# Two attention blocks in fp32 on one core: where a batch of stores is issued, three pair transfers in two attentions, one seam's PSUM copy, and the place of the last normalise

## The chip, the cores and the metric

The kernel runs on 1 core of one Trainium2 chip. The metric is the device time of one execution in microseconds (us). The kernel before took 3185.87 us, the median of 3 runs (3183.12 to 3187.95).

## The reference

Eight images of 512 channels and 32 x 32 pixels go through two attention blocks, one after the other, each with its own weights. All is fp32.

```python
# one block; C = 512, S = 1024 positions, 8 heads of d = 64, 8 groups
xn  = group_norm(x) * gamma + beta
q, k, v = Wq xn + bq, Wk xn + bk, Wv xn + bv          # 512 x 512 each
attn = softmax(q^T k / sqrt(d))                        # per head, 1024 x 1024
out  = attn v
x    = x + Wp out + bp
```

A pair of an image and a block is called a job here; there are 16, numbered n = 0 to 15 in the order image 0 block 0, image 1 block 0, image 0 block 1, image 1 block 1, then images 2 and 3, and so on. Attention n is the attention of job n.

## The kernel before, in words

**Stages.** TensorE goes through job after job: projections, attention, then a seam into the next job. The output projection of job n is done in the seam together with the projections of job n + 1. The 512 x 512 products use a scheme with 7 products in place of 8 (`v_phase`, `deep_phases`, `last_proj`), one level deep for the first two jobs' values and the last output, two levels deep otherwise. For two levels the weights need sums of blocks ("factors"). They are made once: four times, in attentions 0, 1, 2 and 3, `deep_round` loads a weight matrix into one large SBUF tile (tag `deep`, one buffer; the profile calls it `round`), VectorE forms the factors in 4 + 4 additions (L162 to L168), and seven stores of 448 KB (L235) write them to DRAM, from where later jobs load them (`w<-deep`). The tag `deep` is used again by the next holder: in attention 0 by another raw weight load (L157, `raw`), in attentions 1 to 3 by the sums of the next input (L482 to L488).

**Attention.** There are 8 groups, one for each pair of heads (hp) and half of the query positions (sh), and 8 steps in a group, one for each chunk of 128 key positions: 64 steps of about 1.72 us of TensorE. In step i TensorE makes the scores `sc` (L1099) into one of two PSUM buffers, ScalarE the exponential `e` (L1104) into SBUF, and two steps later TensorE the product with the values (L1150, into `po`). The `e` tiles come from a pool of 12 buffers; at step 58 six of these go to the next job's weights.

**The softmax's sums.** The eight exponentials of a group have to be added. The first four are added in two pairs: a GpSimd transfer adds one exponential onto the other in SBUF (L1127, `e<-e`), and VectorE adds the result to `acc` (L1130) five steps after the issue. The other four are added by VectorE alone (L1118, then L1120). In the last group of an attention `pairs` is 0 and all eight are added by VectorE. After a group, `take` copies one half of `po` to SBUF with ScalarE (L1171) and VectorE adds it to the other half, which it reads from PSUM (L1173). With `middle` given, ScalarE copies the second half as well (L1176) and VectorE adds two SBUF tiles (L1178). `reduce` turns `acc` into row sums (L1185). After every second group the sums are gathered over partitions by three small DMAs (`r<-r`, L1208), 7.6 us later inverted (L1212, L1213, ...), written to DRAM and broadcast back (`rd`, L1225; `rb`, L1227), and 16.2 us later multiplied into the outputs (`normalise`, L1242). For the last two groups this is done on VectorE without DMAs, with times of its own.

**Side work.** `chores` and `moves` hang on step numbers: the next job's group norm (its statistics; `groups`, L331 to L341, with the DMAs `dg` and `mr`; the factors `mul` and `off`, L349 to L351; then four normalisations on ScalarE, L356, in attentions 0, 2 and 3 after steps 24, 25, 27 and 28), the sums of its blocks (L423 to L429), the factor steps and the stores above.

**What sets the order.** TensorE, ScalarE and VectorE execute in the order of the program text, with `later` and `advance` as a clock that inserts delayed steps. The queues of SP and GpSimd are ordered by the framework; each is served in order. [...]

**The last seam.** `last_proj` runs for both halves of the positions. Its chain has four PSUM tiles; the fourth product into `z_last` can start when VectorE has added the product before it to `x` (L1064) . The normalise of the last two groups (L1242) and the sums of the second half (L1018 to L1027) stand among those additions in VectorE's queue.

The few lines that place the stores in an attention (`put_round`, in `fast_path`):

```python
at = max(at + 3, 25)
for i, fn in enumerate(stores):
    at = move(at + 1 + i % 2, fn)
```

They give the steps 26, 28, 29, 31, 32, 34 and 35 in attentions 0, 2 and 3, and 30, 32, 33, 35, 36, 38 and 39 in attention 1.

Of the kernel before, what the change touches and what calls it, by code (L numbers as in the profile page):

```python
# [41 lines left out]
FACTOR = {1: A11, 2: A12, 3: S4, 4: A22, 5: S1, 6: S2, 7: S3}  # L42
# [39 lines left out]
def fast_path(  # L82
# [10 lines left out]
    nc = tc.nc  # L93
# [17 lines left out]
    jobs = [(b0 + i, layer) for b0 in range(0, B, 2) for layer in range(2) for i in range(2)]  # L111
# [4 lines left out]
    def later(delay, fn):  # L116
        todo.append((clock[0] + delay, fn))
# [25 lines left out]
    def raw_block(layer, which, i, j):  # L143

        if which == O:
            w, at = wp[layer], 0
        else:
            w, at = wqkv[layer], {Q: 0, K: C, V: 2 * C}[which]
        cols = slice(at + i * CH, at + (i + 1) * CH)
        return w[j * CH : (j + 1) * CH, cols].rearrange("(cc p) o -> p cc o", p=P)  # L150
# [8 lines left out]
    def factor(w, part):  # L159

        if part == 0:
            nc.vector.tensor_add(w[:, S1], w[:, S3], w[:, A22])  # L162
        elif part == 1:
            nc.vector.tensor_sub(w[:, S2], w[:, S1], w[:, A11])
        elif part == 2:
            nc.vector.tensor_sub(w[:, S3], w[:, A11], w[:, S3])
        else:
            nc.vector.tensor_sub(w[:, S4], w[:, A12], w[:, S2])  # L168
# [43 lines left out]
    def deep_round(which, layer):  # L212


        box = []

        def start():
            t = acts.tile([P, NW, NW, P], F32, tag="deep", name=f"round_{which}_{layer}")
            box.append(t)
            for i in range(2):  # L220
                for j in range(2):
                    nc.sync.dma_start(
                        t[:, 2 * j + i, 0:4, :].rearrange("p (cc h) o -> p cc (h o)", cc=2),
                        raw_block(layer, which, i, j),
                    )

        def outer_(part):
            factor(box[0][:, :, 0:4, :], part)

        def inner(part):  # L230
            factor(box[0].rearrange("p f a o -> p a f o"), part)

        def store(o):
            keep = wdram.tile([P, NW, P], F32, name=f"deep_{which}_{layer}_{o}")
            nc.sync.dma_start(keep, box[0][:, FACTOR[o]])  # L235
            deep[which, layer, o] = keep

        first = [lambda part=part: outer_(part) for part in range(4)]
        second = [lambda part=part: inner(part) for part in range(4)]
        return start, first, second, [lambda o=o: store(o) for o in OUTER]  # L240
# [837 lines left out]
    class Attention:  # L1078
# [41 lines left out]
                nc.vector.tensor_add(acc[g], acc[g], e)  # L1120

        def pairs(self, g):
            return 0 if g + 1 == len(self.groups) else 2

        def add_pair(self, i):
            g, kc = self.steps[i]
# [28 lines left out]
        def finish(self, g):  # L1155

            self.take(g)
            if not self.pairs(g):
                self.reduce(g)

# [15 lines left out]
        def reduce(self, g):  # L1180
            n, q, m = self.n, self.q, g % 2
            hp, sh = self.groups[g]
            if m == 0:
                self.r = small.tile([P, NQ, 2, RP], F32, tag="r", name=f"r_{n}_{g}", bufs=1)
            nc.vector.tensor_reduce(  # L1185
                self.r[:, 0, m, :], self.acc.pop(g).rearrange("p j (b e) -> p (j b) e", e=RP), AX.X,
                ALU.add, apply_transpose=True,
            )
            if m == 0:
                return  # L1190
            before = self.groups[g - 1]
            if before[0] == hp:
                place = q[:, hp, :].rearrange("p (m e) -> p m e", m=2)
            else:
                place = q[:, hp - 1 : hp + 1, sh * HALF : (sh + 1) * HALF]
            r, first = self.r, slice(0, RP)
            ends = g + 1 == len(self.groups)
            lt = small.tile([RP, 2, RP], F32, tag="lt", name=f"lt_{n}_{g}", bufs=1)
            ri = small.tile([P, 2, 2, RP // 2], F32, tag="ri", name=f"ri_{n}_{g}", bufs=1)
            box = []  # L1200

            def gather():
                for i in range(1, NQ):
                    src, to_ = r[i * RP : (i + 1) * RP, 0], r[first, i]
                    if ends:
                        nc.vector.tensor_copy(to_, src)
                    else:
                        nc.sync.dma_start(to_, src)  # L1208

            def invert():  # L1210
                inv = ri[first].rearrange("p m j b -> p m (j b)")
                nc.vector.tensor_reduce(lt, r[first].rearrange("p a m b -> p m b a"), AX.X, ALU.add)  # L1212
                nc.vector.reciprocal(inv, lt)  # L1213
                box.append(apool.tile([P, 2, HALF], F32, tag="rb", name=f"rb_{n}_{g}", bufs=1))
                if ends:
                    for i in range(1, NQ):
                        nc.vector.tensor_copy(
                            ri[i * RP : (i + 1) * RP, :, 0, :], ri[first, :, i * RP // HD, :]
                        )
                else:  # L1220
                    rt = small.tile([RP, 2, RP], F32, tag="rt", name=f"rt_{n}_{g}", bufs=1)
                    rd = dram.tile([2, 2, HALF], F32, tag="rd", name=f"rd_{n}_{g}")
                    for i in range(2):
                        nc.vector.transpose(rt[:, i, :], inv[:, i, :])
                    nc.sync.dma_start(rd.rearrange("m j (b e) -> (j b) m e", e=RP), rt)  # L1225
                    for j in range(2):
                        nc.sync.dma_start(  # L1227
                            box[0][j * HD : (j + 1) * HD],
                            rd[:, j, :].unsqueeze(0).to_broadcast([HD, 2, HALF]),
                        )  # L1230
                nc.vector.tensor_max(lmax, lmax, lt)
                nc.vector.tensor_max(rmax, rmax, inv)

            def spread():
                if ends:
                    nc.vector.transpose(
                        box[0].rearrange("p m (b e) -> p m b e", e=RP),
                        ri[:, :, 0, :].unsqueeze(3).to_broadcast([P, 2, RP // 2, RP]),
                    )

            def normalise():
                nc.vector.tensor_mul(place, place, box[0])  # L1242
                whole[0] = n if ends else -1

            times = (0.0, 7.6, 7.7, 16.2)
            if ends:
                times = (0.0, 0.2, 7.6, 8.2) if n + 1 >= DEEP_V else (0.0, 0.2, 2.0, 4.0)
                if n + 1 == len(jobs):
                    times = (0.0, 0.2, 2.0, 7.0)
            for at, step in zip(times, (gather, invert, spread, normalise)):  # L1250
                later(at, step)

# [682 lines left out]
```

## Time and profile before

| | |
|---|---|
| median of 3 runs | 3185.87 us (3183.12 to 3187.95) |
| the profiled execution | 3187.94 us, its span on the core 3186.2 us |
| TensorE busy / idle | 3156.2 / 22.8 us |
| VectorE, ScalarE, GpSimd busy | 2637.2, 2333.5, 281.0 us |
| granted TensorE clock | 0.996 |
| DMA, queues of SP and of GpSimd | 27.4% and 25.8% of 16 engines' span |

All durations in the text are from this one profiled execution. The page gives busy time per engine and groups of instructions by line. The view of waits adds up, for an engine, who ended its idle time. A timeline lists an engine's instructions in order: start and duration in us, engine, line, operation, output and input tiles, and in brackets the idle time before it and what ended that. "SPq" is SP's queue of DMA issues; the time of an issue is not the time of the transfer.

| attention | start (first exponential) | end (last exponential) |
|---|---|---|
| 0 | 81.4 us | 197.8 us |
| 1 | 294.6 us | 402.0 us |
| 2 | 492.6 us | 604.1 us |
| 3 | 692.2 us | 804.7 us |
| 4 | 892.8 us | 1000.3 us |

### The profile page before, as it was taken

The page shows a single profiled execution, that of the slowest core. Times are in us where ns is not written, and L with a number is a line of the kernel's source. Part 1 is how long each engine was busy: PE and PEld are TensorE (multiplying, and loading weights), DVE is VectorE, ACT ScalarE, POOL GpSimd, SP SyncE. Part 2 cuts the span into 40 slices and gives each one's busy share as a digit, 9 for nine tenths or more (in the row PEclk, how much of TensorE's full clock was granted, in tenths as well). Part 3 has the DMA queues.
Part 4 walks back from the last instruction along what each step waited for, and adds up shares of the span by engine and source line. Part 5 has one row for each costly group of instructions (what it writes and reads, how often), then busy time and mean ns, then how long its engine had stood idle before and what let it go on. Part 6 is the DMA issues. An engine that isn't in the chain of part 4 may idle for free.

```text
span 3186.2 us, 62139 instructions
## 1 busy us (share of the span) xinstructions
PE 3156.2 (99%) x24093; PEld 1872.4 (59%) x24093; DVE 2637.2 (83%) x3571; ACT 2333.5 (73%) x4233; POOL 281.0 (9%) x318
## 2 busy tenths in 40 slices
PE   9999999999999999999999999999999999999998
PEld 8357384573846638466393754837557375573844
DVE  8797898978879788797978969889697887978867
ACT  6648687786877868777686776867768687686863
POOL 0101101011010010100001000010000100001000
PEclk9999999999999999999999999999999999999999
DMA  7645675565745455355554545446456463544633
GB/s 276 141 124 160 153 210 140 147 192 128 213 98 146 119 110 167 75 151 159 144 184 88 159 98 138 125 94 181 131 137 182 89 201 63 136 121 96 220 78 78
DMA packets 186190, 450.31 MB, mean 141 GB/s; under 512 B 37928, under 2 KB 54176, under 8 KB 185888
## 3 DMA queue, kind: packets, MB, share of 16 engines
q1 hardware_dynamic: 137040, 296.82, 27.4%
q0 software_dynamic: 48848, 149.44, 25.8%
q8 instruction: 192, 3.15, 0.4%
q14 instruction: 110, 0.90, 0.1%
HBM read 247.41 MB, written 48.17 MB: 93 GB/s over the span
## 4 chain that ended last, share of the span: by engine, by line
PE 81%; DVE 1%; issue 0%; DMA 0%; ACT 0%; SPq 0%; POOL 0%; DVEq 0%; ACTq 0%; POOLq 0%
PE sc L1099 23%; PE po L1150 23%; PE zd L806 9%; PE vd L806 9%; PE yd L806 4%; PE ud L806 4%; PE vd L801 4%; PE zd L801 3%; PE yd L801 1%; PE ud L801 1%; DVE acc L1120 0%; PE z_last L1042 0%; DMA r<-r 0%; ACT e L1104 0%; DVE x L1064 0%
## 5 line engine op out<-in xcount | busy, mean ns | idle before, releaser
L1104 ACT ACTIVATE e<-sc 128x1024 f32<-128x1024 f32 x1024 | 1043.8, 1025 | 575.6 <-PE sc L1099 546.9
L1099 PE MATMUL sc<-q,k 64*64 64x512 f32 x8192 | 1059.2, 590 | 10.1 <-ACT e L1104 10.1
L1150 PE MATMUL po<-e,v 64*64 64x512 f32 x8192 | 1058.0, 590 | 3.4 <-ACT e L1104 3.4
L1099 PEld LDWEIGHTS sc<-q,k 64*64 64x64 f32 x8192 | 309.6, 133 | 576.7 <-issue 509.9
L1150 PEld LDWEIGHTS po<-e,v 64*64 64x64 f32 x8192 | 311.6, 133 | 572.6 <-issue 544.2
L1120 DVE TENSOR_TENSOR acc<-acc,e 128x1024 f32<-128x1024 f32 x320 | 389.4, 1217 | 39.1 <-ACT e L1104 28.9
L1127 POOL DMA_DIRECT2D e<-e x224 | 192.9, 861 | 1769.0 <-ACT e L1104 1267.8
L1118 DVE TENSOR_TENSOR acc<-e,e 128x1024 f32<-128x1024 f32 x128 | 156.4, 1222 | 147.1 <-ACT e L1104 147.1
L1130 DVE TENSOR_TENSOR acc<-acc,e 128x1024 f32<-128x1024 f32 x224 | 272.4, 1216 | 1.9
L806 PE MATMUL zd<-deep,w 128*128 128x256 f32 x860 | 240.2, 379 | 0.0
L806 PE MATMUL vd<-deep,w 128*128 128x256 f32 x804 | 223.4, 379 | 0.0
L806 PEld LDWEIGHTS zd<-deep,w 128*128 128x128 f32 x860 | 163.3, 190 | 22.5 <-ACT ud L501 0.3
L806 PEld LDWEIGHTS vd<-deep,w 128*128 128x128 f32 x804 | 152.8, 190 | 20.8
L1185 DVE TRANSPOSE_TENSOR_REDUCE r<-acc 128x32 f32<-128x1024 f32 x128 | 159.4, 1245 | 4.3
L901 POOL DMA_DIRECT2D x<-p x61 | 72.9, 1195 | 972.9 <-ACT p L823 453.9
L848 DVE TENSOR_TENSOR p<-p,s 128x512 f32<-128x512 f32 x185 | 127.2, 687 | 22.8 <-ACT p L823 19.3
L801 PE MATMUL vd<-w,deep 128*128 128x128 f32 x840 | 119.1, 275 | 1.1 <-ACT ud L501 1.1
L848 DVE TENSOR_TENSOR q<-q,s 128x512 f32<-128x512 f32 x64 | 44.1, 690 | 86.8 <-ACT q L825 45.1
L801 PE MATMUL zd<-w,deep 128*128 128x128 f32 x728 | 106.5, 275 | 0.9 <-ACT ud L501 0.9
L801 PEld LDWEIGHTS vd<-w,deep 128*128 128x128 f32 x840 | 106.2, 192 | 1.3 <-ACT ud L501 1.3
L806 PE MATMUL vd<-os,w 128*128 128x256 f32 x364 | 105.5, 379 | 0.0
L806 PE MATMUL zd<-os,w 128*128 128x256 f32 x356 | 98.9, 379 | 0.0
(296 smaller groups left out, 4826.4 us busy)
## 6 DMA issues: line engine op xcount, KB each, us to landing
w<-deep SPq DMA_DIRECT2D x399, 448.0 KB, 5.4
e<-e POOLq DMA_DIRECT2D x224, 512.0 KB, 4.7
x<-p POOLq DMA_DIRECT2D x61, 512.0 KB, 6.6
rb<-rd SPq DMA_DIRECT2D x96, 256.0 KB, 3.7
x<-x_dram SPq DMA_DIRECT2D x28, 512.0 KB, 3.7
out_dram<-x SPq DMA_DIRECT2D x28, 512.0 KB, 6.0
deep<-w SPq DMA_DIRECT2D x28, 448.0 KB, 2.7
deep<-round SPq DMA_DIRECT2D x28, 448.0 KB, 4.9
```

Of the source, the lines that this page charges most:

```text
L801: nc.tensor.matmul(ps[:, tokens], moving[i][:, tokens], lhs[:, FACTOR[i], :], start=(start and ti == 0), stop=True, skip_group_check=True,)
L806: nc.tensor.matmul(ps, lhs[:, FACTOR[i], :], moving[i], start=start, stop=True, skip_group_check=True,)
L848: nc.vector.tensor_add(to_, to_, five.to_broadcast([P, 2, QT]))
L901: nc.gpsimd.dma_start(to_, p(part), accum_op=ALU.add)
L1099: nc.tensor.matmul(sc[h * HD : (h + 1) * HD, j, :], k[r, hp, k0 : k0 + HD], q[r, hp, sh * HALF : (sh + 1) * HALF], start=True, stop=True,)
L1104: nc.scalar.activation(e, sc, AF.Exp, scale=SCALE)
L1118: nc.vector.tensor_add(acc[g], self.es[i - 1], e)
L1120: nc.vector.tensor_add(acc[g], acc[g], e)
L1127: nc.gpsimd.dma_start(self.summed[i], self.summed.pop(i - 1), accum_op=ALU.add)
L1130: nc.vector.tensor_add(self.acc[g], self.acc[g], self.summed.pop(i))
L1150: nc.tensor.matmul(po[g][j * HD : (j + 1) * HD, h, :], v[r, kc, d0 : d0 + HD], e[r, j, :], start=(kc == 0), stop=(kc == NT - 1),)
L1185: nc.vector.tensor_reduce(self.r[:, 0, m, :], self.acc.pop(g).rearrange("p j (b e) -> p (j b) e", e=RP), AX.X, ALU.add, apply_transpose=True,)
```

## The change

1. The 28 stores of `deep_round` are issued from ScalarE's queue, at their place in ScalarE's order between exponentials, in place of SP's queue.
2. In attentions 0 and 1, groups 1 to 4, three pairs are added by transfers in place of two: 8 more `e<-e` transfers; in each of these groups one L1130 more and two L1120 fewer. The reduce of these groups, and what hangs on it, comes two steps later.
3. At the end of attention 0 (the one seam where `finish` is called for the last group and another job follows), both halves of `po` are copied by ScalarE, and VectorE adds two SBUF tiles.
4. In the last seam the normalise is placed at 9.6 us of the program's clock in place of 7.0.

In the built program TensorE's order is unchanged. ScalarE's gains the 28 stores and one copy. In VectorE's, attentions 0 and 1 change: in attention 0 the factors L349 to L351 now stand before the inverse L1212. In SP's queue of attention 0 the order r<-r, seven stores, raw, rd, raw x3, rb x2, r<-r becomes r<-r, rd, rb x2, r<-r, raw x4, rd, rb x2. In the last seam L1242 moves behind the additions of `y_last` and `z_last`.

```diff
@@ deep_round, store
-            nc.sync.dma_start(keep, box[0][:, FACTOR[o]])
+            nc.scalar.dma_start(keep, box[0][:, FACTOR[o]])
@@ Attention
         def pairs(self, g):
-            return 0 if g + 1 == len(self.groups) else 2
+            if g + 1 == len(self.groups):
+                return 0
+            return 3 if self.n < 2 and 0 < g < 5 else 2
@@ finish
-            self.take(g)
+            if not self.pairs(g) and self.n + 1 < len(jobs):
+                self.take(g, lambda: None)
+            else:
+                self.take(g)
             if not self.pairs(g):
                 self.reduce(g)
@@ reduce
                 if n + 1 == len(jobs):
-                    times = (0.0, 0.2, 2.0, 7.0)
+                    times = (0.0, 0.2, 2.0, 9.6)
```

## The prediction

> **What bounds the kernel now.** I read the page's busy times first, then who TensorE waited for, then the time order of each engine around each wait.
>
> ```profile
> PE 3156.2 (99%) x24093; PEld 1872.4 (59%) x24093; DVE 2637.2 (83%) x3571; ACT 2333.5 (73%) x4233; POOL 281.0 (9%) x318
> ```
>
> TensorE is busy 3156 of 3186.2 us and nothing here removes a matmul. All that can be won is its idle time, 22.8 us. The waits of TensorE name nearly all of it:
>
> ```profile
> PE sc L1099 <- ACT e L1104: 10.1, 4, 3.4
> PE po L1150 <- ACT e L1104: 3.4, 1, 3.4
> PE v L553 <- DVE q L1173: 2.8, 1, 2.8
> ...
> PE z_last L1042 <- DVE x L1064: 1.3, 1, 1.3
> PE vd L801 <- ACT ud L501: 1.1, 1, 1.1
> PE zd L801 <- ACT ud L501: 0.9, 1, 0.9
> ```
>
> In order of time, from TensorE's timeline: S1 3.36 us at 128.4 (attention 0); S2 3.36 at 197.9 (its last step), 0.23 behind it; S3 2.77 at 209.1 (first seam); S4 0.86 and 1.09 at 416 and 421 (second seam); S5 3.00 and 0.58 at 539 (attention 2); S6 3.19 at 739 (attention 3); S7 1.34 at 3164.9 (last seam). The first 9 us hold the other 3.
>
> S1, S5 and S6 read "waits for an exponential", but the exponential stood behind a normalisation, and that behind VectorE. In the answer for L356:
>
> ```profile
> its engine sat idle before it (us, times) until:
>   DVE off L351: 12.6, 3
> ```
>
> VectorE in attention 0, at S1:
>
> ```profile
> 122.86 0.59 DVE L1212 TENSOR_REDUCE lt<-r 32x64 f32<-32x256 f32 x1 [3.10 <-DMA r<-r]
> ...
> 124.53 1.21 DVE L1120 TENSOR_TENSOR acc<-acc,e 128x1024 f32<-128x1024 f32 x1
> 125.67 0.14 DVE L349 TENSOR_TENSOR mul<-mr,vec_sb 128x4 f32<-128x4 f32 x1
> ```
>
> The factors L349 to L351 are queued behind L1212, which stands still until the gather r<-r lands. The same sequence stands at S5 and S6. Now SP's queue and the VectorE wait that follows:
>
> ```profile
> 116.69 1.84 SPq L1208 DMA_DIRECT2D r<-r  x3
> 118.58 7.85 SPq L235 DMA_DIRECT2D deep<-round  x7
> 131.17 0.38 SPq L157 DMA_DIRECT2D raw<-wqkv_dram  x1
> 131.61 0.46 SPq L1225 DMA_DIRECT2D rd<-rt  x1
> 132.11 1.45 SPq L157 DMA_DIRECT2D raw<-wqkv_dram  x3
> 134.16 2.26 SPq L1227 DMA_DIRECT2D rb<-rd  x2
> ```
>
> ```profile
> 146.70 1.23 DVE L1242 TENSOR_TENSOR q<-q,rb 128x1024 f32<-128x1024 f32 x1 [14.70 <-DMA rb<-rd]
> ```
>
> Seven stores are issued, then SP stands until they have landed (raw reuses their buffer), and rd and rb stand behind that. VectorE loses 14.7 us. I measured its lag as the start of a group's first sum (L1118) after the second exponential it reads: 0.4 us in group 1 of attention 0, 11.9 in group 3, 11.8 still in group 7 (start 195.48, exponential ended 183.65). In attention 1 it is 5.2 us at group 7, later at most 2.7. Twelve us of lag make S2: the last exponential needs the buffer which that sum frees.
>
> ```profile
> 196.79 1.02 ACT L1104 ACTIVATE e<-sc 128x1024 f32<-128x1024 f32 x1 [4.62 <-DVE acc L1118]
> ```
>
> [...] r<-r lands 0.45, 0.5 and 0.2 us after the GpSimd pair transfer then in flight (122.29, 533.09, 733.23).
>
> **The change, part by part.**
>
> *Stores by ScalarE, attention 0.* In the built order rd and rb now stand before raw, and raw comes one group later. rd is ready about 127, rb about 132 to 133 (typical landing 3.7 us), VectorE reaches L1242 at about 131. The 14.7 us wait falls to 0 to 3. What is late next is raw: the last store is issued after exponential 35, about 141, lands about 146 (median 4.9 us), raw lands about 150 to 153, VectorE wants it at about 152. A lag of 2 to 5 us is left. S2 needs a lag over about 8.5 (11.8 minus the stall 3.36). So S2 goes: -3.4, and the 0.23 behind it, -0.2; this would hold without the pairs.
>
> *Three pairs in attentions 0 and 1, groups 1 to 4.* Each adds one transfer and one L1130 and drops two L1120: one add of 1.22 us fewer, eight in all, 9.8 us of VectorE, beside TensorE. What counts is the order: group 1's reduce and its inverse move two steps (3.4 us) later, so L349 to L351 now stand ahead of L1212. They follow the group's first sum, whose exponential ends at 120.2: 120.2 + 1.2 + 0.6 = 122.0, and ScalarE wants them at 121.8. S1 goes. ScalarE then has exponentials (0.91 start to start), four normalisations (1.14) and a copy (0.46) between steps 24 and 29: by this addition exponential 26 starts 1.4 us after its scores, and TensorE bears 1.5 (2.58 us from scores to reuse, less 1.06). I take 0.15 left of 3.36: -3.2. Transfers take 25.8% of 3186 us over 285 (224 + 61), 2.9 us of all DMA engines each; three pairs in a group of 13.75 us are 63%, the stores (27.4% of 3186 us for 297 MB, so 1.35 us each) some 60% of the 15.5 us they are spread over. So for that stretch DMA is full, and transfers land up to 5 us late. A pair is wanted 5 steps, 8.6 us, after issue and lands in 4.7; its buffer is wanted 5 steps later still. That covers 5 us; if the cover is gone, each further us stops VectorE, then TensorE.
>
> *The same in attention 1.* The lag before the deep sums falls from 4.4 to about 3.5 us; the stores end at step 39, so L482, which overwrites their buffer at 42, need not wait. S4 comes from VectorE freeing small buffers late, so 0.9 less lag takes 0.8 of 1.95; bounds 0 and 2. The first store waits for the last factor step (346.56 before, about 344.5 now) and is due after exponential 30, 345.4: no wait taken. If it came 2 us later, exponential 31 behind it would be late and TensorE after it.
>
> *Attentions 2 and 3.* VectorE's order is the same, so L349 stays behind L1212. The stores stood behind r<-r on SP, not before it; they can only slow its landing. r<-r landed 1.8 and 3.9 us after its last issue; in attentions 4 to 13, with no store near, 1.2 to 5.0, mostly 3.2. [...] So S5 gives 0.1, S6 0.4: -0.5; bounds -2 (r<-r's whole wait) and 0.
>
> *Issue cost on ScalarE.* On SP a store took:
>
> ```profile
> L235 SPq DMA_DIRECT2D deep<-round x28: 353/730/1330, 118.6 to 738.9; - x28
> ```
>
> The 1330 belongs to back-to-back issue, now they are 2 to 3 us apart. [...] Behind a store stand the next exponential, then TensorE. In attentions 0, 2 and 3 ScalarE has from step 26 to 35 10 x 1.72 - 10 x 0.905 - 2 x 1.14 - 0.46 = 5.4 us to spare for seven. Lower bound 0 [...]; at the median 0.73 wholly exposed, the bunch at steps 26 to 29 costs 1.2 us in each, 3.7; no gain is possible. I take 0.2 each: +0.6.
>
> *First seam.* S3 is a PSUM bank held by L1173, which stood behind five L1120. A ScalarE copy (0.58 us, ScalarE is idle 2.9 us there) now frees it: -2.8. With the lag gone L1173 would have been early anyway. VectorE's later sums there are not later than before.
>
> *Last normalise.* L1242 (1.13 start to start) stood before the x<-y_last and x<-z_last that free the bank:
>
> ```profile
> 3162.11 1.20 DVE L1242 TENSOR_TENSOR q<-q,rb 128x1024 f32<-128x1024 f32 x1
> 3163.24 0.85 DVE L1064 SCALAR_TENSOR_TENSOR x<-y_last,out_bias,x 128x256 f32<-128x256 f32 x2
> 3164.02 0.85 DVE L1064 SCALAR_TENSOR_TENSOR x<-z_last,out_bias,x 128x256 f32<-128x256 f32 x2
> 3164.80 0.67 DVE L1018 TENSOR_TENSOR t_last<-q 128x512 f32<-128x512 f32 x1
> ```
>
> It moves behind both: the bank is free 1.13 earlier, -1.1. Its own reader in TensorE starts at 3166.8 - 1.1 = 3165.6, L1242 ends at about 3164.9; L1018 starts as before. Cover 0.7 us.
>
> **Sum.** -3.2 - 3.4 - 0.2 - 2.8 - 0.8 - 0.5 - 1.1 + 0.6 = -11.4 us, against the profiled execution, 3187.94 (span 3186.17, 1.8 around it). That one is 2.1 over the median of 3185.87. From the median: 3174.5.
>
> **Rivals.**
> - S5 and S6 go too, because the stores were what held r<-r. For it: they follow it at once on the same queue. Against: the 3.2 us without stores, and the order of L349. A further -6.3: 3168.2.
> - Attention 0 keeps its lag, since stores, three pairs, raw and rb meet in full DMA engines. For it: rb took 12 us in such company. S2 and S4 stay: -11.4 + 4.4, 3178.9.
> - Issue at 1.1 us, exposed: 7.7 - 5.4 = 2.3, with the bunch 2.5 in three attentions, 7.5 in place of 0.6: 3181.4.
> - Slower: ScalarE is stopped by its own stores. One SP issue (r<-r at 557.7) took 1.9 us. At 1.9: 13.3 - 5.4 - 0.1 (lag that TensorE still bears) = 7.8 us in each of three attentions, 4.2 in attention 1 (9.1 to spare): 27.6 - 12.0 = +15.6, 3201.5. It decides from 1.34 us an issue (break even), 1.57 for 0.2% slower. Against it: spacing[...].
>
> **How the numbers follow.** A measurement tells about 0.2%, 6.4 us, from no change: faster is under 3179.5. Chances: forecast 0.60 (3172 to 3178), S5 and S6 too 0.10, lag kept 0.15, issue at 1.1 us 0.10, slower 0.05. Faster 0.60 + 0.10 + 0.14 = 0.84; same 0.11; slower 0.05. From 3170 to 3182 about 0.15 is left out: half of the second case, half of the fourth, the last.
>
> **What would show it.** Right: no wait of L1242 for rb over 4 us in attention 0, lag at its group 7 under 6 us; L349 before the inverse there; L356's idle time three times down to two, about 8 us; TensorE's L553 wait gone; z_last's under 0.4. Wrong: exponentials that start late right after a store; a wait on e<-e over 5 us on VectorE; S5 or S6 under 1.5 us, which would say that the stores did hold r<-r.

## The result, and the profile after

The changed kernel takes 3188.0 us, the median of 22 runs (3183.8 to 3190.9), beside 3185.5 us before (22 runs, 3179.1 to 3188.0). The ratio is 1.0009, with a 95% interval of 1.0002 to 1.0015. The forecast gain of 11.4 us is not there; the kernel is, if anything, 2.5 us slower. That is within the 0.2% that the prediction took for no change. The profiled execution took 3189.4 us, its span is 3187.6.

The change adds lines, so from here on the same instructions carry other numbers: from L1127 on they are 2 higher (L1130 is now L1132), from L1171 on 5 higher (L1173 is now L1178, L1212 is L1217, L1242 is L1247), and 3 more in k_thin.

TensorE's busy time and VectorE's, on the page after:

```profile
PE 3155.9 (99%) x24093; PEld 1873.2 (59%) x24093; DVE 2628.9 (82%) x3563; ACT 2334.8 (73%) x4234; POOL 290.8 (9%) x326
```

VectorE has lost 8.3 us of work (the forecast had 9.8), but TensorE is idle for 26.2 us where it was idle for 22.8. The view of TensorE's waits after (who was waited for: us in total, times, longest):

```profile
PE sc L1099 <- ACT e L1104: 9.1, 4, 2.9
PE po L1152 <- ACT e L1104: 5.1, 2, 4.1
PE zd L806 <- ACT yd L497: 3.2, 1, 3.2
PE zd L801 <- ACT ud L501: 2.3, 1, 2.3
PE z L553 <- DVE v L579: 2.2, 1, 2.2
...
PE z_last L1042 <- DVE x L1064: 0.2, 1, 0.2
```

The wait at `v` L553 (S3) is gone, and that at `z_last` (S7) is nearly gone. The rest has changed places. In order of time:

| place | before, us | after, us |
|---|---|---|
| S1, factors of attention 0, near 128 | 3.36 | 2.92 + 0.58 |
| S2, end of attention 0 | 3.36 + 0.23 | 1.06 + 0.68 |
| S3, first seam, near 209 | 2.77 | 0 |
| first seam, 219 and 244 | 0 | 2.17 + 3.16 |
| end of attention 1, 403 | 0 | 4.08 |
| S4, second seam | 0.86 + 1.09 | 2.34 |
| S5 | 3.00 + 0.58 | 2.88 |
| S6 | 3.19 | 2.70 |
| S7, last seam | 1.34 | 0.19 |

**What stands in place of rb's long wait.** VectorE's timeline in attention 0, cut to the lines that wait 1 us or more for a transfer:

```profile
124.80 0.16 DVE L349 TENSOR_TENSOR mul<-mr,vec_sb 128x4 f32<-128x4 f32 x1 [3.74 <-DMA mr<-dg]
...
137.72 1.23 DVE L1247 TENSOR_TENSOR q<-q,rb 128x1024 f32<-128x1024 f32 x1 [4.27 <-DMA rb<-rd]
147.59 1.23 DVE L1132 TENSOR_TENSOR acc<-acc,e 128x1024 f32<-128x1024 f32 x1 [1.11 <-DMA e<-e]
157.85 0.59 DVE L1217 TENSOR_REDUCE lt<-r 32x64 f32<-32x256 f32 x1 [4.10 <-DMA r<-r]
...
171.26 1.22 DVE L1247 TENSOR_TENSOR q<-q,rb 128x1024 f32<-128x1024 f32 x1 [4.35 <-DMA rb<-rd]
```

The single wait of 14.7 us has become several of 1 to 4 us, and they add up to nearly as much: the lag at group 7 of attention 0 is 9.5 us (11.8 before). The windows of the trace show how full the DMA engines were meanwhile (window, its length, busy time of TensorE, weight loads, VectorE, ScalarE and GpSimd, then clock, DMA share and GB/s), first before, then after:

```profile
140.00:155.00 15.00, 15.00 (x145) 5.00 (x140) 8.16 (x8) 9.31 (x10) 1.74 (x2) 1.00 0.75 136
155.00:170.00 15.00, 15.00 (x148) 4.99 (x140) 14.73 (x20) 9.82 (x12) 1.74 (x2) 1.00 0.39 73
```

```profile
140.00:155.00 15.00, 15.00 (x144) 5.36 (x140) 12.47 (x12) 9.94 (x11) 2.62 (x3) 1.00 1.06 268
155.00:170.00 15.00, 15.00 (x144) 5.36 (x140) 8.25 (x14) 9.79 (x11) 1.74 (x2) 1.00 0.98 222
```

In attention 1 the lag rose from 5.2 to 12.6 us:

```profile
326.08 0.69 DVE L162 TENSOR_TENSOR round<-round 128x512 f32<-128x512 f32 x1 [5.03 <-DMA round<-wqkv_dram]
349.20 1.23 DVE L1247 TENSOR_TENSOR q<-q,rb 128x1024 f32<-128x1024 f32 x1 [2.67 <-DMA rb<-rd]
366.80 0.60 DVE L1217 TENSOR_REDUCE lt<-r 32x64 f32<-32x256 f32 x1 [5.08 <-DMA r<-r]
377.93 1.23 DVE L1247 TENSOR_TENSOR q<-q,rb 128x1024 f32<-128x1024 f32 x1 [3.00 <-DMA rb<-rd]
```

**Why S1 is still there.** As planned, L349 now stands ahead of the inverse (L1217). But it waits 3.74 us for `mr`. The chain behind `mr` begins with GpSimd's pow (L336), and GpSimd's timeline shows it took 4.6 us:

```profile
111.58 4.62 POOL L336 TENSOR_TENSOR ga<-gv,neg_half 8x1 f32<-8x1 f32 x1 [4.35 <-DVE gv L335]
116.16 1.50 POOL L1129 DMA_DIRECT2D e<-e  x2
```

SP issues the store of its result (`dg`) at 116.22, as soon as it ends. In the same place it took 1.48 us before, and its median over the kernel is 0.56. Now VectorE's timeline over the same time:

```profile
111.42 1.21 DVE L1132 TENSOR_TENSOR acc<-acc,e 128x1024 f32<-128x1024 f32 x1
112.56 1.07 DVE L164 TENSOR_TENSOR round<-round 128x896 f32<-128x896 f32 x1
113.56 1.07 DVE L166 TENSOR_TENSOR round<-round 128x896 f32<-128x896 f32 x1
114.56 1.21 DVE L1132 TENSOR_TENSOR acc<-acc,e 128x1024 f32<-128x1024 f32 x1
115.80 1.25 DVE L1190 TRANSPOSE_TENSOR_REDUCE r<-acc 128x32 f32<-128x1024 f32 x1
```

Four additions of two SBUF tiles stand in a row, from 111.42 to 115.77 us, and the pow ends at 116.20, 0.4 us after the first instruction with one input (L1190) starts. In the kernel before only one such addition lies between L335 and the reduce (L1185 there), from 111.83 to 113.04 us, and the pow takes 1.48 us, to 113.47, and also ends 0.4 us after the start of the reduce. So in both traces the pow ended only when the row of additions had, and in after it did not get in between the four. By what means they hold it the traces do not show; m_groups16 below is the run that takes them away from its start.

**What a stall costs beside its length.** The windows of the trace give the granted clock of TensorE. These are after's windows around its longest stall:

```profile
398.00:402.00 4.00, 0.73 (x8) 0.00 (x0) 3.97 (x5) 0.26 (x1) 0.00 (x0) 1.00 0.52 137
402.00:406.00 4.00, 3.18 (x15) 1.70 (x16) 3.97 (x5) 1.53 (x3) 0.00 (x0) 0.64 1.01 372
406.00:410.00 4.00, 4.00 (x35) 4.00 (x35) 3.79 (x4) 3.36 (x10) 0.00 (x0) 0.94 0.97 336
```

After the stall TensorE runs at a lower clock, 0.64 and 0.94 in these windows: 4 x 0.36 + 4 x 0.06 = 1.7 us are lost though it is busy. The length of the stall alone does not decide it: in these two profiles the clock fell after stalls of 2.34 to 4.08 us, and it did not after others of 2.92 (S1 in after), 3.00 (S5 in before) and 3.16 us (the first seam in after). What decides is not tested. I summed (1 - clock) over all windows of 2 us. Before lost 1.7 us behind each of S1, S2, S3 and S6, 6.8 in all; after lost it behind the stalls at 403 and 420 and behind S5 and S6, also 6.8. (The first 20 us are left out: there the lost clock was 3.4 us in the profile of before and none in that of after, in a stretch which the change does not touch.) So idle time and lost clock after the first 20 us are 19.8 + 6.8 = 26.6 us before and 23.1 + 6.8 = 29.9 after: 3.3 more, against 2.5 more in the medians. This sum is used for all experiments below. It is not the whole of the time: what remains when it is taken from the profiled execution lies between 3157.5 and 3162.2 us over the kernels below, so a difference in cost of a few us is no proof by itself.

### The profile page after: what moved, and what is told of

Same layout as the page of the kernel before. It is cut to its first block, busy times and chain, and to the rows that moved or that the text cites. A ratio compares the mean times of both kernels' runs of the same rounds, so it can differ in the third digit from the quotient of the medians.

```text
span 3187.6 us, 62162 instructions
## 1 busy us (share of the span) xinstructions
PE 3155.9 (99%) x24093; PEld 1873.2 (59%) x24093; DVE 2628.9 (82%) x3563; ACT 2334.8 (73%) x4234; POOL 290.8 (9%) x326
## 3 DMA queue, kind: packets, MB, share of 16 engines
q1 hardware_dynamic: 133008, 283.98, 26.2%
## 4 chain that ended last, share of the span: by engine, by line
PE 76%; DVE 1%; issue 0%; ACT 0%; DVEq 0%
PE sc L1099 22%; PE po L1152 21%; PE zd L806 8%; PE vd L806 8%; PE yd L806 4%; PE ud L806 3%; PE vd L801 3%; PE zd L801 3%; PE yd L801 1%; PE ud L801 1%; DVE acc L1120 0%; PE z_last L1042 0%; DVE acc L1132 0%; DVE x L1064 0%; PE y_last L1042 0%
## 5 line engine op out<-in xcount | busy, mean ns | idle before, releaser
L1120 DVE TENSOR_TENSOR acc<-acc,e 128x1024 f32<-128x1024 f32 x304 | 370.1, 1217 | 38.2 <-ACT e L1104 28.5
L1129 POOL DMA_DIRECT2D e<-e x232 | 199.6, 860 | 1766.6 <-ACT e L1104 1460.3
L1132 DVE TENSOR_TENSOR acc<-acc,e 128x1024 f32<-128x1024 f32 x232 | 282.4, 1217 | 3.1 <-DMA e<-e 1.1
L1190 DVE TRANSPOSE_TENSOR_REDUCE r<-acc 128x32 f32<-128x1024 f32 x128 | 159.4, 1245 | 4.3
L848 DVE TENSOR_TENSOR p<-p,s 128x512 f32<-128x512 f32 x185 | 127.5, 689 | 27.1 <-ACT p L823 21.2
L848 DVE TENSOR_TENSOR q<-q,s 128x512 f32<-128x512 f32 x64 | 44.2, 691 | 86.5 <-ACT q L825 45.1
```

The lines of the kernel that those rows point to most:

```text
L848: nc.vector.tensor_add(to_, to_, five.to_broadcast([P, 2, QT]))
L1129: nc.gpsimd.dma_start(self.summed[i], self.summed.pop(i - 1), accum_op=ALU.add)
L1132: nc.vector.tensor_add(self.acc[g], self.acc[g], self.summed.pop(i))
L1190: nc.vector.tensor_reduce(self.r[:, 0, m, :], self.acc.pop(g).rearrange("p j (b e) -> p (j b) e", e=RP), AX.X, ALU.add, apply_transpose=True,)
```

## Experiments

"Cost" is TensorE's idle time plus lost clock after the first 20 us of the profiled execution; "lag" is the prediction's measure, at group 7 of attentions 0 and 1. Each median is of 5 to 22 runs, each cost and lag of one profile. Ratios are to the kernel before, run on the same chip (3185.3 to 3185.9).

| kernel | median, us | ratio, 95% interval | cost, us | lag 0 / 1, us |
|---|---|---|---|---|
| before | 3185.5 | 1 | 26.6 | 11.8 / 5.2 |
| changed | 3188.0 | 1.0009 (1.0002 to 1.0015) | 29.9 | 9.5 / 12.6 |
| a_stores | 3181.9 | 0.999 (0.9981 to 0.9998) | 21.6 | 3.2 / 9.0 |
| b_pairs | 3195.5 | 1.0035 (1.0021 to 1.0048) | 36.6 | 5.5 / 10.5 |
| c_seams | 3185.0 | 0.9997 (0.9989 to 1.0005) | 23.3 | 9.6 / 4.5 |
| d_no_pairs | 3181.1 | 0.999 (0.9982 to 0.9998) | 19.8 | 1.8 / 9.0 |
| e_factors | 3172.7 | 0.9962 (0.9948 to 0.9976) | 13.8 | 5.5 / 9.0 |
| f_att1_sp | 3178.7 | 0.9978 (0.9972 to 0.9985) | 16.5 | 5.5 / 3.9 |
| g_pairs45 | 3185.6 | 1.0002 (0.9994 to 1.0011) | 21.0 | 1.7 / 9.0 |
| h_both | 3167.3 | 0.9952 (0.9938 to 0.9966) | 7.9 | 5.5 / 4.4 |
| i_pairs0 | 3167.7 | 0.9948 (0.9934 to 0.9961) | 7.8 | 9.0 / 4.0 |
| j_pairs1 | 3172.5 | 0.9965 (0.9951 to 0.9978) | 11.4 | 5.5 / 10.6 |
| k_thin | 3185.5 | 1.0001 (0.9993 to 1.001) | 25.8 | 5.3 / 9.8 |
| l_seam | 3160.8 | 0.9926 (0.9913 to 0.994) | 2.3 | 5.5 / 4.5 |
| m_groups16 | 3182.3 | 0.9988 (0.9981 to 0.9995) | 22.5 | 8.9 / 12.4 |
| n_pairs45 | 3164.6 | 0.9937 (0.9924 to 0.9951) | 2.5 | 5.5 / 4.4 |

The lag of attention 0 moves by itself. In d_no_pairs and f_att1_sp attention 0 is the same program, and it is 1.8 and 5.5 us: the same broadcast `rb`, issued at 158.65 and 158.82 us, kept VectorE waiting 1.10 and 4.12 us. In before and c_seams, again the same program up to the end of attention 0, it is 11.8 and 9.6. A single difference under 4 us in that column therefore says nothing. Groups of kernels do: with the third pair in attention 0 and the stores on ScalarE it is 8.9 to 9.5 us, without the pair 1.7 to 5.5. In attention 1 kernels with the same program agree within 1 us.

### The parts one by one

**a_stores.** Only part 1.

```diff
-            nc.sync.dma_start(keep, box[0][:, FACTOR[o]])
+            nc.scalar.dma_start(keep, box[0][:, FACTOR[o]])
```

> Only the stores are moved to ScalarE; two pairs everywhere, seams as before. Theory (the third pair fills the DMA engines and gives the gain back): without it rb comes in time, VectorE's lag at group 7 of attention 0 is under 6 us, the stall S2 (3.36 us) and the low-clock time behind it (1.7 us) go, no new stall at 402 or 420; 4 to 8 us faster than before, 3178 to 3182. Rival (the stores, spread over 15 us by ScalarE, delay what follows by themselves): lag 9 us or more at group 7 with two pairs too, within 2 us of before or slower. Rival (absorption: VectorE's debt is paid somewhere in the first seam whatever is done): S2 gone, but 2 to 5 us of new waits between 205 and 250; 3183 to 3187.

The lag of attention 0 is 3.2 us, S2 and its lost clock are gone, and S3 with them. But attention 1's lag rose to 9.0 us and a stall of 2.93 us with lost clock came at 397, where the theory had none. The time, 3181.9, is just inside its range. The theory holds for attention 0; what showed in attention 1 is the rival's mechanism, stores that delay what follows.

**b_pairs.** Only part 2.

```diff
-            return 2
+            return 3 if self.n < 2 and 0 < g < 5 else 2
```

> Only the third pair in attentions 0 and 1; stores on SP, seams as before. Theory (pairs fill the DMA engines): attention 1 shows a lag of 9 us or more at group 7 (before 5.2, after 12.6) and the new stall near 402; attention 0 keeps a lag over 10 us; 2 to 10 us slower than before, 3187 to 3195. Rival (the spread stores are what delays): attention 1's lag falls below 5 us as the sums saved would have it, no stall near 402; 3180 to 3185.

9.9 us slower than before, 0.5 over the range. Attention 1's lag is 10.5, as the theory said, and stalls of 2.0 and 1.7 us came at 405 and 408. In attention 0 the stores and `raw` still stood in SP's queue before `rd` and `rb`, and VectorE waited longer than before (its timeline, and SP's queue):

```profile
153.00 1.22 DVE L1247 TENSOR_TENSOR q<-q,rb 128x1024 f32<-128x1024 f32 x1 [19.62 <-DMA rb<-rd]
```

```profile
123.38 7.43 SPq L235 DMA_DIRECT2D deep<-round  x7
134.82 2.07 SPq L157 DMA_DIRECT2D raw<-wqkv_dram  x4
136.93 1.69 SPq L1230 DMA_DIRECT2D rd<-rt  x1
145.48 1.30 SPq L1232 DMA_DIRECT2D rb<-rd  x2
```

TensorE stood 7.1 us at 159 for it. The lag at group 7 is 5.5 us, not over 10 as expected: TensorE itself had been held back by then. S1 stayed here too (2.94 us), with the stores still on SP.

**c_seams.** Only parts 3 and 4 (the seam's copy, 9.6 in place of 7.0).

> Only the copy of the seam and the later last normalise; stores on SP, two pairs. Both theories: the last seam gains 1.1 us. First seam: if the bank was all that was late, S3 (2.77) and its low-clock time (1.7) go: 5.6 us faster in all, 3180. Absorption: VectorE's lag of 11.8 us is still there, so a wait of 2 to 3 us comes back at L579 some 10 us later: 1 to 3 us faster, 3182.5 to 3184.5.

S3 and S7 are gone, yet the time cannot be told from before. TensorE's waits show where S3 went:

```profile
PE zd L806 <- ACT yd L497: 3.1, 1, 3.1
PE z L553 <- DVE v L579: 2.0, 1, 2.0
```

These are the new stalls of the changed kernel at 244 and 219. Absorption was right, and gave back 0.5 us more than its range: VectorE came into the seam 10 us late, and TensorE, no longer held at 209, met it ten and thirty-five us later. At the second place ScalarE stood 4.09 us for a transfer `x<-p`, which GpSimd had issued 0.55 us after an addition by VectorE into a `p` tile (L848); l_seam below takes this transfer out.

**d_no_pairs.** The change without part 2.

> The change without the third pair: stores on ScalarE, seam copy, later last normalise. Theory (pairs give the gain back): S2 and S3 go with their low-clock times, S7 shrinks, S1 stays: idle and low-clock time 8 to 12 us less than before; 3173 to 3178. Rival (spread stores delay): lag at group 7 of attention 0 stays over 9 us, 3183 to 3188. Absorption: 3180 to 3184.

Better than the changed kernel by 6.9 us, with the lag of attention 0 at 1.8 us. It misses 3173 to 3178 because of attention 1, as in a_stores, where TensorE waited 2.7 us for `w<-deep` with 1.7 of lost clock behind it. S1, expected to stay, cost 3.3 us and 1.7 of clock:

```profile
PE sc L1099 <- ACT e L1104: 10.0, 4, 3.3
PE vd L801 <- DMA w<-deep: 2.7, 1, 2.7
```

### Attention 1, and S1, S5, S6

**f_att1_sp.** d_no_pairs, with attention 1's stores back on SP.

```diff
-            nc.scalar.dma_start(keep, box[0][:, FACTOR[o]])
+            (nc.sync if (which, layer) == ROUNDS[1] else nc.scalar).dma_start(
+                keep, box[0][:, FACTOR[o]])
```

> Without the third pair, and the stores of attention 1 alone back on SP; those of 0, 2 and 3 on ScalarE. Theory (in attention 1 the stores, issued one by one by ScalarE up to the gather r<-r of group 3, make that and rb land late; on SP they are done 7 us before it): lag at group 7 of attention 1 from 8.9 back to about 5 us, the stalls at 393 and 396 (3.1 us and 1.7 of low clock) go, 0.9 to 2 us come back at 414 to 421 as before: 2 to 4 us less than the kernel without pairs, 3177 to 3179. Rival (the lag of attention 1 has nothing to do with the stores): no difference, 3181.

As expected in attention 1: the lag is 3.9 us, its stalls are gone, 1.0 us came back at 412. (A stall of 3.2 us at 241, in the first seam, is new; l_seam below deals with it.) In d_no_pairs the seven stores ran from 336.2 to 349.4 us, up to the gather r<-r, which SP issued at 349.6; VectorE then waited 4.26 us for it and 2.05 for `rb`. On SP they come in one bunch, all issued 7 us before the gather (from 339.5 to 346.1 us, r<-r at 353.0), and VectorE waited 1.23 us for it.

**e_factors.** d_no_pairs, with the group statistics and the factors one step earlier in attentions 0, 2 and 3.

```diff
-                        at = (17, 23, 24, 25, 27, 28, 30, 32, 34, 36)
+                        at = (16, 22, 24, 25, 27, 28, 30, 32, 34, 36)
```

> Without the third pair, and in attentions 0, 2 and 3 the group statistics and the factors L349 to L351 one step earlier, so that the factors stand before the inverse L1217 and its wait for r<-r. Theory (S1, S5, S6 are VectorE's order: factors behind an inverse that waits): all three go, with their low-clock times; the kernel without pairs had 3.3 + 3.7 + 3.0 us there and 3.4 of low clock: 10 to 13 us less, 3168 to 3171. Rival (mr<-dg lands with the pair transfer [...], so the factors wait as long): they shrink by 2.5 us at most each, 3173 to 3177. Rival (four normalisations and the exponentials do not fit ScalarE's time): 1.5 us stays in each.

S1, S5 and S6 are gone, all three, with nothing left. VectorE's timeline in attention 0:

```profile
121.05 0.16 DVE L349 TENSOR_TENSOR mul<-mr,vec_sb 128x4 f32<-128x4 f32 x1
121.54 0.59 DVE L1217 TENSOR_REDUCE lt<-r 32x64 f32<-32x256 f32 x1
```

So neither the stores nor ScalarE's load made them. The edit moves two things, the statistics and the factors; for S5 and S6 m_groups16 below tells them apart. The time is 1.7 us over the range, because a stall of 3.1 us with 3.4 of lost clock came in the first seam:

```profile
PE zd L806 <- ACT yd L497: 3.1, 1, 3.1
```

**h_both.** Both edits.

> Without the third pair, factors one step earlier, stores of attention 1 on SP. If both reasons hold, what the two single runs gain adds: 3165 to 3169. If TensorE, now earlier, meets VectorE later on (absorption), a third or more of it comes back: 3171 to 3175.

The gains add up: 3167.3 us, inside the range. Taken by themselves they are 8.4 and 2.4 us, which would give 3170.3, so nothing came back.

**l_seam.** h_both, with the first partial sum `x<-p` of the first seam added by VectorE and not by a GpSimd transfer.

```diff
-                    more(0, 0, 2, True)
+                    more(0, 0, 2, m > 0)
```

> The base (3167.3), with the first x<-p of the first seam added by VectorE in place of a transfer. Theory (TensorE's stall at 237.9, 3.3 us and 1.7 of low clock, is ScalarE waiting for that transfer to leave its p tile): it goes, 4 to 5 us faster, 3162 to 3164. Rival (the second transfer or VectorE, 1.2 us later, takes its place): within 2 us of the base.

In h_both ScalarE stood at the tile that this transfer reads (ScalarE's timeline):

```profile
237.07 0.47 ACT L825 ACTIVATE p<-yd,out_step 128x256 f32<-128x256 f32 x1 [4.26 <-DMA x<-p]
```

With the addition on VectorE the stall is gone and nothing took its place: 3160.8 us, 1.2 below the range and 24.7 us under the kernel before. (The stall at 73 us also happened to be 0.7 us in place of 1.4.) All of TensorE's waits over 0.5 us that are left:

```profile
PE first_y L1391 <- POOL blk L76: 1.5, 1, 1.5
PE vd L801 <- ACT ud L501: 1.1, 1, 1.1
PE pm L374 <- DVE mv L283: 0.8, 2, 0.6
PE zd L806 <- ACT ud L501: 0.7, 1, 0.7
PE pvar L386 <- DVE mr L382: 0.6, 1, 0.6
```

### The third pair: bytes or order?

**k_thin.** The changed kernel, but the third pair's transfer moves an eighth of the bytes.

```diff
+            to_, src = self.summed[i], self.summed.pop(i - 1)
+            if kc == 5:
+                to_, src = to_[:, 0, :P], src[:, 0, :P]
-            nc.gpsimd.dma_start(self.summed[i], self.summed.pop(i - 1), accum_op=ALU.add)
+            nc.gpsimd.dma_start(to_, src, accum_op=ALU.add)
```

> The changed kernel with all four parts, but the third pair's transfer adds only 128 of the 1024 columns (64 KB in place of 512), so that sums of attentions 0 and 1 lack the rest; every engine's order is that of the changed kernel. Theory (bytes: the engines of the DMA are full): lag at group 7 of attention 0 from 9.5 to 5 us or less, of attention 1 from 12.6 to 9 or less, the stall near 128 shrinks or goes; 3170 to 3179. Rival (order: the reduce two steps later and one more issue in GpSimd's queue): lags of 9 us and 12 us stay, 3185 to 3190.

Both answers are partly right. The lags fell to 5.3 and 9.8 us, what the kernels without a third pair, with the stores on ScalarE, have (1.7 to 5.5, and 9.0): the bytes made the pair's share of the lag. S1 stayed, at 2.94 us with 1.7 of clock, and so did the pow and the wait for `mr`:

```profile
111.31 4.62 POOL L336 TENSOR_TENSOR ga<-gv,neg_half 8x1 f32<-8x1 f32 x1 [4.38 <-DVE gv L335]
```

```profile
124.54 0.16 DVE L349 TENSOR_TENSOR mul<-mr,vec_sb 128x4 f32<-128x4 f32 x1 [3.75 <-DMA mr<-dg]
```

So S1 is order. The time, 3185.5, is above what I gave the theory: apart from S1, the stall at 241 (3.1) is there as in the other kernels that have the seam's copy and a lag of 5.3 us or more, and every one of its five long stalls at 127, 241, 415, 539 and 739 was followed by lost clock, 8.6 us in all.

**m_groups16.** The changed kernel; only the group statistics one step earlier.

```diff
-                        at = (17, 23, 24, 25, 27, 28, 30, 32, 34, 36)
+                        at = (16, 23, 24, 25, 27, 28, 30, 32, 34, 36)
```

> The changed kernel with all four parts; only the group statistics L331 to L336 of attentions 0, 2 and 3 come one step earlier, the factors stay where they were. Theory (GpSimd's pow is held by VectorE's additions of two SBUF tiles; the factors then wait for mr): pow 0.6 us in place of 4.6, the wait of 3.7 us at L349 and TensorE's stall near 128 go; S5 and S6 stay; the lag of attention 0 after that stays near 9 us: 3 to 6 us faster than the changed kernel, 3182 to 3185. Rival (mr is late because it lands with the pair transfers): mr lands at 124 all the same, stall stays, 3188.

GpSimd's and VectorE's timelines:

```profile
110.61 0.56 POOL L336 TENSOR_TENSOR ga<-gv,neg_half 8x1 f32<-8x1 f32 x1 [3.13 <-DVE gv L335]
```

```profile
121.23 0.15 DVE L349 TENSOR_TENSOR mul<-mr,vec_sb 128x4 f32<-128x4 f32 x1
```

The pow is back at 0.56 us, L349 waits for nothing and runs at 121.2, where the prediction had put it (122.0), and S1 is gone. The earlier start alone would have brought 1 us of the 3.74 that L349 waited; the shorter pow brings 4.1.

The kernel is 5.7 us faster than the changed one, but S1 is not all of that. S5 and S6, expected to stay, fell from 2.9 and 2.7 to 1.7 us each, and the lost clock behind both is gone. The traces show the reason. In SP's queue r<-r stands behind `mr`, which needs the statistics. In attention 2 of the changed kernel the reduce ends at 529.4 and r<-r is issued at 533.0; here it ends at 526.25 and r<-r is issued at 526.28, and the inverse no longer waits (VectorE, changed kernel, then this one):

```profile
537.39 0.59 DVE L1217 TENSOR_REDUCE lt<-r 32x64 f32<-32x256 f32 x1 [1.63 <-DMA r<-r]
```

```profile
532.54 0.59 DVE L1217 TENSOR_REDUCE lt<-r 32x64 f32<-32x256 f32 x1
```

The 1.7 us that stay are VectorE's order, since e_factors, which also moves the factors, has none.

**i_pairs0 and j_pairs1.** h_both, with the third pair in attention 0 alone, and in attention 1 alone.

```diff
-            return 2
+            return 3 if self.n < 1 and 0 < g < 5 else 2     # i_pairs0
+            return 3 if self.n == 1 and 0 < g < 5 else 2    # j_pairs1
```

> The kernel with early factors and attention 1's stores on SP (3167.3), with the third pair in attention 0 alone. Theory (third pairs meet the stores, raw, rb in full DMA engines): lag at group 7 of attention 0 from 5.5 to 9 us or more, a stall of 1 us or more at its end or at the factors; 4 to 9 us slower, 3171 to 3176. Rival (once the factors stand right, eight fewer additions only help): lag 5 us or less, 3164 to 3168.

> The same base (3167.3), with the third pair in attention 1 alone. Theory: lag at group 7 of attention 1 from 4.4 to 9 us or more, 2 to 4 us of stall at 393 to 400 with 1.7 us of low clock; 3170 to 3174. Rival (in attention 1 it was the spread stores, not the pairs): lag 5 us or less, 3165 to 3168.

Attention 1 is as the theory said, 5.2 us slower, with its lag at 10.6 and stalls of 2.1 and 1.9 us at its end. In attention 0 the lag is 9.0, as forecast, but the time did not move (3167.7, expected 3171 to 3176). In its profile the end and the seam give 0.5 + 1.3 + 1.5 us of new waits, while the stall of 0.6 to 1.4 us at 74 and the 1.7 of lost clock in the seam are absent. Why the median of five runs agrees with the base stays open. A longer lag is a cost only where a stall follows, and the theory had priced it as if it always did.

**g_pairs45 and n_pairs45.** The third pair in attentions 4 and 5, where nothing is stored: on d_no_pairs, then on l_seam.

```diff
-            return 2
+            return 3 if self.n in (4, 5) and 0 < g < 5 else 2
```

> The third pair in attentions 4 and 5, where nothing is stored, in place of 0 and 1. Theory (the third pair does harm where it meets the stores and the loads of the weight rounds): lag in attentions 4 and 5 stays under 4 us, no new wait of TensorE there, VectorE 9.8 us less busy, time as without pairs, 3179 to 3183. Rival (it does harm by itself: the transfers keep VectorE's small gathers waiting, or the later reduce shifts the order): lag over 6 us or new waits at 1000 or 1200, 3184 or more.

> The fastest kernel so far (3160.8: no third pair in 0 and 1, early factors, attention 1's stores on SP, seam addition on VectorE) with the third pair in attentions 4 and 5, away from any store. Theory (away from stores it costs nothing that counts): 3160 to 3162, lags of attentions 4 and 5 under 5 us. Rival (it costs by itself): 3163 to 3166, with waits of TensorE in or after attentions 4 and 5.

The lag at group 7 stays at 3.8 us or less in those attentions, so it is the company of a weight round that makes it 10. A round has stores, loads and VectorE's factor additions; which of them counts is not separated here. But the pair does not come free: 4.5 and 3.8 us slower than their bases (3181.1 and 3160.8), each in another series of runs; the second pair's ratio intervals overlap. The profile of n_pairs45 places 1.5 us: the starts of attentions 4 to 6 are 196.7 and 196.0 us apart, in l_seam 195.6. Where the rest lies stays open. The 9.1 us of work that it saves VectorE are worth nothing where VectorE is not waited for.

## Why the prediction was wrong, point by point

These are the terms of the forecast's sum beside what the two profiles show, in us:

| term | forecast | idle time | lost clock |
|---|---|---|---|
| S1 | -3.2 | +0.1 | -1.7 |
| S2 and the wait behind it | -3.6 | -1.9 | -1.7 |
| first seam (S3) | -2.8 | +2.6 | -1.7 |
| end of attention 1, S4 | -0.8 | +4.5 | +3.4 |
| S5, S6 | -0.5 | -1.2 | +1.7 |
| last seam | -1.1 | -1.1 | 0 |
| issue on ScalarE | +0.6 | none seen | |
| a wait at 73 us | none | +0.3 | 0 |
| sum | -11.4 | +3.3 | 0 |

S1, the first seam and the end of attention 1 failed, each by a step of its own: `mr` was taken to be there, a stall was booked as removed while VectorE stayed late, and full DMA engines were priced at nothing.

- **Stores, attention 0: right by itself, wrong in company.** "A lag of 2 to 5 us is left. So S2 goes" is what a_stores and d_no_pairs show (3.2 and 1.8; S2 gone). With the third pair beside it 9.5 us are left. The sentence that failed is "That covers 5 us". It saw that the DMA engines would be full (share 1.06 and 0.98 from 140 to 170 us), but weighed the lateness against the pairs' own cover only. That held: VectorE stood 1.11 us for e<-e. But it executes in order and stands on the smaller transfers as well: 4.27, 4.10 and 4.35 us for rb (256 KB), r<-r (8 KB) and rb. The rival "attention 0 keeps its lag", at 0.15, had this mechanism. The threshold of 8.5 us of lag for S2 was right: 9.5 us left a stall of 1.06, 9.0 us (i_pairs0) 0.51. That S2 shrank is not shown to be the change's doing, as c_seams, with attention 0 as before, has 1.15 us there.
- **S1: the order came out as predicted, the time did not.** "120.2 + 1.2 + 0.6 = 122.0" assumed that `mr` was there. It came at 124.7, behind a pow of 4.62 us. I listed what the third pair moves in VectorE's queue, and did not ask which engine has to wait while those additions run. m_groups16 shows the term: with the pow at 0.56 us and `mr` in time, the 3.5 us of S1 are gone.
- **Attention 1: wrong in sign.** "The lag before the deep sums falls from 4.4 to about 3.5 us." The additions saved are there, but two things outweigh them: stores spread up to the gather behind them (f_att1_sp: 5.0 us of lag) and the pairs (j_pairs1: 6.2 us of lag; k_thin: 2.8 us of it go with the bytes when both are there). For this part I asked whether the last store hinders L482, not what it does to r<-r and rb, due at the same time. 4.08 and 2.34 us of stall, with 1.7 us of clock behind each, came where 0.8 was to be gained.
- **First seam: S3 removed, its cause not.** "VectorE's later sums there are not later than before" is true on the clock and wrong as an argument: TensorE comes 2.8 us earlier, with 1.7 less of lost clock, and meets the same sums. c_seams gives it all back (2.0 and 3.1 us).
- **S5 and S6: right within the bounds.** They gave 0.7 and 0.5 us (0.1 and 0.4 forecast). The stores left SP's queue and both stayed, so the rival "the stores held r<-r" is out. Most of their cause is the one named, L349 behind the inverse: 1.7 us of each (m_groups16, e_factors). The other 1.2 and 1.0 us were r<-r behind `mr` in SP's queue. S5 now carries lost clock that it did not before.
- **Issue on ScalarE: right at the lower bound.** 0.6 was taken, and no exponential is seen to start late behind a store. ScalarE's timeline, and the group of the stores:

```profile
136.47 1.02 ACT L1104 ACTIVATE e<-sc 128x1024 f32<-128x1024 f32 x1 [0.49 <-ACT e L1104]
136.50 0.33 ACTq L235 DMA_DIRECT2D deep<-round  x1
```

```profile
L235 ACTq DMA_DIRECT2D deep<-round x28: 326/326/658, 125.6 to 759.9; - x28
```

  An issue takes 0.33 us (0.66 once), and 27 of the 28 start while an exponential or a normalisation runs. ScalarE's waits after them, 0.16 to 0.90 us, are all for TensorE's scores. That an issue can lie under the running instruction was the prediction's lower bound, and after's trace shows it. The slower rival rested on SP's 1.9 us, which ScalarE never showed.
- **Last seam: right.** 1.34 became 0.19 us.
- **A cost that the working did not have at all.** Each stall was priced at its length. Behind S1, S2, S3 and S6 stood 1.7 us of lost clock each, and behind four stalls of after too. It does not change the balance of this change (6.8 both times), but it made single gains and losses 1.7 us larger than I priced them. It also breaks the first step, "All that can be won is its idle time, 22.8 us": l_seam is 24.7 us faster, and TensorE's busy time fell from 3156.2 to 3147.5 us in it.

Of the signs that the prediction named for itself, the order of L349, the end of the wait at L553 and the last seam came true. The wait for rb (4.27 us), the lag (9.5) and L356's idle time (11.4 us, still three times) did not.

In all, the stores in attention 0, the last seam, S5 and S6 and the issue cost were right taken one at a time. The third pair (b_pairs) and the stores in attention 1 (a_stores) were wrong by themselves: a late r<-r, rb or `mr` had no price. And at the first seam a stall was taken as removed when only its place was.

## What to carry to other kernels

When two parts of a change fill the same stretch of a shared resource, cost them together, and do so for every transfer that an in-order engine waits for, the smaller ones too, as r<-r (4.10 us) and rb (4.27 and 4.35) were here. Before a stall is booked as a gain, ask by how much the late engine is late: if its lag stays, the fast engine can meet it at the next place, as in c_seams (2.77 us gone, 2.0 and 3.1 new). And when work moves in VectorE's order, look at what GpSimd has to do at that moment as well (the pow: 4.62 us in place of 0.56), and at what the next transfer in an in-order queue stands behind (r<-r behind `mr`: issued 3.6 us after its reduce in place of 0.03).

## What the runs showed of the hardware that was not expected

- A GpSimd operation on 8 x 1 elements took 0.56 (m_groups16), 1.48 (before) or 4.62 us (after), as none, one or four additions of two SBUF tiles stood in a row in VectorE from its start on.
- Clock was lost in portions of 1.70 to 1.72 us, or twice that. A stall of 2.3 us (at 420 in the changed kernel) cost one, and one of 2.9 us (at 127.6) none, so the length alone does not decide. What does stays open.
- A DMA issue of 448 KB took 0.33 us on ScalarE (0.66 once), where SP took 0.35 to 1.33 for the same stores, issued in bunches.
- Seven stores of 448 KB issued over 13 us, up to a small gather, in place of 7 us ending 7 us ahead of it, cost VectorE 5 us of lag in attention 1 (d_no_pairs against f_att1_sp).
